# Five fixed PSUM places, earlier additions of finished sums, and means multiplied on GpSimd, in a graph network kernel

## The chip, the cores and the metric

The kernel runs on one core of one Trainium2 chip. The metric is device time in microseconds (us) of one execution. The kernel before took 1561.95 us, the median of three runs (1561.57 to 1563.52). A core has five engines that each work through their own queue in order: TensorE (PE; PEld is its weight load), VectorE (DVE), ScalarE (ACT), GpSimd (POOL) and SyncE (SP). They meet only through semaphores. Lines such as L1570 are lines of the kernel before; the change moves later lines down by 19 to 27.

## What is computed

A graph with 6250 nodes (64 features, `x`) has 206,250 directed edges (64 features each), sorted by destination `dst`; `src` says to which node an edge's message is added.

```python
msg = concat([x[dst], edge_attr], axis=1)          # 206250 x 128
h = relu(msg @ W1a.T + b1a) @ W1b.T + b1b          # 128, then 64
sums = segment_sum(h, src, 6250); counts = segment_sum(1, src, 6250)
agg = sums / maximum(counts, 1)
z = relu(concat([x, agg]) @ W2a.T + b2a) @ W2b.T + b2b
out = layernorm(x + concat([z, x]) @ Wr.T + br)    # no scale, eps 1e-5
```

All of it is float32. Because the second linear layer of the messages commutes with the mean, the kernel sums the 128 hidden values per node and applies the product `W1b`, `W2a` once per node.

## The kernel before

The 206,250 edges make 124 blocks of 13 tiles (a tile is 128 edges). For each block TensorE makes the hidden rows of its edges (`hidden`, L1385) into PSUM, and ScalarE applies the relu and writes them to an output row buffer `orow` in SBUF (L1389), a ring of four blocks. VectorE and TensorE meanwhile count, with one-hot matrices of bins (a bin is 128 nodes, there are 49), where each edge's row belongs in a large table `rows` in DRAM (`counts_of`, `bins_of`, `slots`). GpSimd then scatters each tile's 128 rows with one indirect DMA (`ones_`, L1436). In blocks 4 to 109 two or three times three tiles are "joined": edges of the same bin are put in fours (`marks` L1253, L1258, L1259, `join` L1288, `join_rows` L1300), and one indirect DMA writes 128 fours (`fours`, L1408). A block so takes 13, 9 or 7 scatters. Blocks 0 to 109 are epoch 0, then follow epoch 1 (12 blocks, 110 to 121) and epoch 2 (blocks 122 and 123), each with its own table; scatters of block k are issued after block k+2 is written in the program.

As soon as tiles of `rows` are full, SyncE reads them back (`read`, L1516) into a ring of nine buffers `rt`. VectorE makes one-hot matrices of the nodes (`nodes_of`, L1550), and TensorE sums a group of up to three bins with matmuls of 128x129 (`summed`, L1570) into one PSUM tile `g.ps`: the first half of a group in `sum_first`, the rest in `sum_rest`. The sums are added to `part` in SBUF by `collect(n)`, which leaves the n youngest finished groups for later: a first sum of a bin is copied by ScalarE (L1639), a later one is added by VectorE (L1641). In a joined block `sum_first` and `sum_rest` lie at both ends of the `join`, and `collect(0)` stands in the middle, behind `join_bases` on VectorE.

All PSUM tiles called `h_ps` come from one pool of five buffers, `hp`: hidden rows, joins, sums, and the products of the last rounds. A tile is requested under the same name each time and the pool hands out one of the buffers.

What is left after block 123 runs in this order: the sums of epoch 1, then the "last rounds": 17 groups of up to three bins, whose rows of epoch 2 are read and summed, with seven stages a group that are staggered over seven rounds. In round i the program handles `means` of group i-1 (VectorE, L1962 and L1963: one over the count), `scaled` i-1 (ScalarE, L1969: three scalings of 128x128), `turned` i-2 (three transposes on TensorE, L1976, and a copy by ScalarE, L1978), `layer` i-3 (TensorE L1982, VectorE maximum L1983), `residual` i-4 (TensorE L1988, VectorE add L1990), `squares` i-5 (ScalarE, L1997, three with a running sum), `written` i-6 (ScalarE root L2002, VectorE reciprocal L2003, multiply on GpSimd or, for the last two groups, on VectorE, L2006; SyncE stores it, L2011 and L2015), and the sums of group i. Six rounds without sums drain the stages.

The orders of TensorE, VectorE, ScalarE and SyncE are those of the program (`manual_schedule`, closed after the last rounds); GpSimd's is set by the framework. In blocks 9 to 122 most scatters also wait for a point that TensorE must have reached in the next block (`PACED`, `done`). At the very end a flag decides whether a general path runs; it doesn't here.

Of the kernel before, what the change touches and what calls it, by code (L numbers as in the profile page):

```python
# [8 lines left out]
F32 = mybir.dt.float32  # L9
# [4 lines left out]
AF = mybir.ActivationFunctionType  # L14
# [463 lines left out]
FULLQ = (3, 6, 9, 11, 13)  # L478
NODES = 8


# [7 lines left out]
def fast_path(  # L489
# [274 lines left out]
    with (  # L764
        tc.tile_pool(name="orow", bufs=1) as op,
        tc.tile_pool(name="oh", bufs=3) as ohp,
        tc.tile_pool(name="slotp", bufs=1, space=PSUM) as slpp,
        tc.tile_pool(name="hps", bufs=5, space=PSUM) as hp,
    ):
        by_slot = ctx.enter_context(ExitStack())  # L770
        rp = by_slot.enter_context(tc.tile_pool(name="rhs", bufs=1))
# [858 lines left out]
        def collect(n):  # L1630

            while len(totals) > n:
                g = totals.pop(0)
                to = part[:, g.b0 : g.b0 + g.nb, :]
                bins_ = range(g.b0, g.b0 + g.nb)
                assert len({b in begun for b in bins_}) == 1
                if g.b0 not in begun:
                    begun.update(range(g.b0, g.b0 + g.nb))
                    nc.scalar.copy(to, g.ps[:, : g.nb, :])  # L1639
                else:  # L1640
                    nc.vector.tensor_add(to, to, g.ps[:, : g.nb, :])  # L1641

        def sum_first(k):
# [4 lines left out]
            halves.append(g)  # L1648
            g.ps = hp.tile([P, SUMS, H + 1], F32, name="h_ps")
            g.half = range(g.b0, g.b0 + -(-g.nb // 2))  # L1650
# [122 lines left out]
        for k, ep_ in enumerate(epoch_of):  # L1773
# [11 lines left out]
            if joined(k):  # L1785
                marks(k, 0)
            if k == 1:
                join_consts()
# [21 lines left out]
            if after:  # L1810
                join_bases(k + 1)
            if joined(k):
                collect(0)
            for i in range(1, joined(k)):
# [133 lines left out]
        with tc.tile_pool(name="nw2", bufs=2) as nw2, tc.tile_pool(name="nw", bufs=3) as nw, tc.tile_pool(  # L1948
# [3 lines left out]
            class Nodes:  # L1952
# [13 lines left out]
                def scaled(self):  # L1966
                    self.agg = nw2.tile([P, SUMS, H], F32, name="agg")
                    for j in range(self.nb):
                        nc.scalar.activation(  # L1969
                            self.agg[:, j, :], part[:, self.b0 + j, :H], AF.Copy, scale=self.rc[:, j : j + 1]  # L1970
                        )

# [20 lines left out]
                def squares(self):  # L1993
                    self.ssq = nw.tile([P, SUMS], F32, name="ssq")
                    for j in range(self.nb):
                        sq = nw2.tile([P, D], F32, name="sq")
# [136 lines left out]
```

## Time and profile before

| what | value |
|---|---|
| median of three runs | 1561.95 us |
| the profiled execution | 1562.71 us |
| its span in the trace | 1560.9 us |
| TensorE busy | 1435.2 us, 92% |
| VectorE busy | 1369.4 us, 88% |
| GpSimd busy | 1134.2 us, 73% |
| ScalarE busy | 1120.6 us, 72% |
| mean granted TensorE clock | 0.972 |

The span begins with the first instruction and ends with the last; the execution's own time has 1.8 us around it. Busy time leaves out the issue of instructions, so an engine at 73% can be without a free moment: whether it is, the timeline tells, not the share. The chain of waits, which follows the end back to what released it, names TensorE for 64% of the span and DMA for 13%; it takes at each step one releaser and so says nothing of how much slack the others had. A group of the profile has count, busy us and mean ns, and the idle time ahead of it with what ended it.

### The profile page before, as it was taken

What the parts mean: (1) busy time and instruction counts of PE and PEld (TensorE: products, weight loads), DVE (VectorE), ACT (ScalarE), POOL (GpSimd) and SP (SyncE); (2) the same over time, 40 slices, a digit from 0 to 9 for tenths busy, and PEclk for the clock granted to TensorE, in tenths of its full rate; (3) what the DMA queues carried; (4) which work ended last, traced back from release to release, by engine and by line L of the source; (5) the groups of instructions that cost most, each with busy time, mean ns of one, the idle gap of its engine ahead of it and who ended that gap; (6) DMA issues with size and microseconds to landing.
All of it is one profiled execution on the core that took longest, in us unless ns stands there. A gap on an engine that the chain in (4) does not pass through costs nothing.

```text
span 1560.9 us, 33538 instructions
## 1 busy us (share of the span) xinstructions
PE 1435.2 (92%) x10958; PEld 1273.7 (82%) x10958; DVE 1369.4 (88%) x3031; ACT 1120.6 (72%) x2336; POOL 1134.2 (73%) x1215
## 2 busy tenths in 40 slices
PE   6688898879999899899998999999999999999896
PEld 5567777758888788788887888898888899999785
DVE  7589998979999899889998999999999888876786
ACT  3279999979888788787888878887877743432036
POOL 5777777777777777777777777777777777777711
PEclk9699999989999999999999999999999999999998
DMA  8878888868887888787787777676787899998873
GB/s 208 235 233 270 266 268 263 259 223 264 264 259 231 250 260 261 206 247 236 217 251 216 223 220 250 206 246 215 218 260 241 255 340 352 325 351 265 260 231 92
DMA packets 248713, 387.83 MB, mean 248 GB/s; under 512 B 43285, under 2 KB 180311, under 8 KB 248527
## 3 DMA queue, kind: packets, MB, share of 16 engines
q1 hardware_dynamic: 167661, 220.81, 50.4%
q0 software_dynamic: 47904, 122.68, 21.8%
q10 hardware_dynamic: 32962, 42.08, 8.1%
q8 instruction: 90, 1.47, 0.4%
q14 instruction: 96, 0.79, 0.2%
HBM read 214.09 MB, written 171.32 MB: 247 GB/s over the span
## 4 chain that ended last, share of the span: by engine, by line
PE 64%; DMA 13%; DVE 8%; ACT 7%; issue 4%; POOL 2%; SPq 0%; ACTq 0%; DVEq 0%; POOLq 0%
PE h_ps L1570 24%; PE h_ps L1288 13%; PE h_ps L1385 10%; PE h_ps L1300 8%; DMA rows<-orow,rowidx 8%; POOL rows L1436 2%; DMA rt<-rows 2%; DMA rows<-orow,qidx 1%; DVE marks L1253 1%; ACT marks L1258 1%; DVE oh L1550 1%; PE cnt_ps L1113 1%; ACT orow L1303 1%; PE cnt_ps L1114 1%; ACT orow L1389 1%
## 5 line engine op out<-in xcount | busy, mean ns | idle before, releaser
L1436 POOL DMA_INDIRECT rows<-orow,rowidx x922 | 898.7, 975 | 292.1 <-issue 143.0
L1570 PE MATMUL h_ps<-rt,oh 128*128 128x129 f32 x3952 | 487.3, 277 | 35.6 <-DVE oh L1550 9.9
L1570 PEld LDWEIGHTS h_ps<-rt,oh 128*128 128x128 f32 x3952 | 469.7, 193 | 49.6 <-issue 12.8
L1550 DVE TENSOR_TENSOR oh<-ramp,rt 128x768 f32<-128x768 bf16 (+4 forms) x391 | 308.2, 825 | 37.4 <-DMA rt<-rows 36.5
L1253 DVE TENSOR_TENSOR marks<-quad_ramp,ramp 128x1024 fp32r<-128x1024 f32 x230 | 276.6, 1209 | 0.0
L1408 POOL DMA_INDIRECT rows<-orow,qidx x230 | 224.0, 974 | 71.0 <-issue 25.9
L1385 PE MATMUL h_ps<-mv,rhs 124*128 124x128 f32 x1844 | 265.6, 289 | 4.4 <-ACT orow L1389 4.4
L1389 ACT ACTIVATE orow<-h_ps 128x512 f32<-128x512 f32 (+1 forms) x266 | 143.5, 539 | 173.5 <-PE h_ps L1385 163.8
L1288 PE MATMUL h_ps<-marks,side 128*128 128x512 f32 x690 | 261.7, 408 | 0.6 <-ACT mv L1354 0.6
L1300 PE MATMUL h_ps<-mv,rj 128*128 128x130 f32 x1840 | 236.7, 281 | 11.0 <-ACT orow L1389 7.4
L1385 PEld LDWEIGHTS h_ps<-mv,rhs 124*128 124x128 f32 x1844 | 233.2, 198 | 6.0 <-ACT orow L1389 4.6
L1288 PE MATMUL h_ps<-marks,rest 128*64 128x512 f32 x690 | 235.3, 395 | 0.0
L1300 PEld LDWEIGHTS h_ps<-mv,rj 128*128 128x128 f32 x1840 | 220.7, 193 | 16.9 <-ACT orow L1389 10.1
L1292 ACT COPY rj<-h_ps 128x512 f32<-128x512 f32 x230 | 131.5, 588 | 92.9 <-PE h_ps L1288 92.4
L1288 PEld LDWEIGHTS h_ps<-marks,side 128*128 128x128 f32 x690 | 131.0, 190 | 50.9 <-issue 2.1
L1259 ACT ACTIVATE marks<-marks,ones 128x512 fp32r<-128x512 f32 x230 | 166.1, 722 | 7.5
L1258 ACT ACTIVATE marks<-quad_ramp,z_act 128x512 fp32r<-128x512 f32 x230 | 166.0, 722 | 0.3 <-DVE z_act L1164 0.3
L1303 ACT ACTIVATE orow<-h_ps 128x260 f32<-128x260 f32 x460 | 151.4, 388 | 8.7 <-PE h_ps L1300 4.3
L1071 DVE TENSOR_TENSOR_SCAN had<-ramp,bins 128x400 bf16<-128x400 bf16 (+2 forms) x124 | 128.5, 1036 | 19.8 <-ACT bins L1092 6.4
L1338 ACT ACTIVATE rhs<-rhs,from_win 60x896 f32<-60x896 bf16 (+2 forms) x116 | 123.8, 1067 | 2.9
L1340 ACT ACTIVATE rhs<-rhs,ones 60x896 f32<-60x896 f32 (+2 forms) x116 | 123.5, 1065 | 2.9
L1288 PEld LDWEIGHTS h_ps<-marks,rest 128*64 128x64 f32 x690 | 93.7, 136 | 38.1 <-issue 0.6
(195 smaller groups left out, 1603.4 us busy)
## 6 DMA issues: line engine op xcount, KB each, us to landing
rt<-rows SPq DMA_DIRECT2D x194, 390.0 KB
rt<-rows SPq DMA_DIRECT2D x97, 325.0 KB
rows<-padrow ACTq DMA_DIRECT2D x24, 1040.0 KB
rhs<-in_edgeT SPq DMA_DIRECT2D x88, 224.0 KB
enat<-in_edgeJ SPq DMA_DIRECT2D x88, 192.0 KB
rows<-orow,rowidx POOLq DMA_INDIRECT x922
rt<-rows SPq DMA_DIRECT2D x40, 260.0 KB
rt<-rows SPq DMA_DIRECT2D x48, 195.0 KB
```

The lines of the kernel that those rows point to most:

```text
L1253: nc.vector.tensor_tensor(m[:, :n, :], all_q[:, None, :].to_broadcast([P, n, QUAD * P]), z[:, :n, None].to_broadcast([P, n, QUAD * P]), op ...
L1258: nc.scalar.activation(m[:, t, :], all_q, AF.Square, bias=z_acts[k][:, i * JOIN + t : i * JOIN + t + 1], scale=-1.0)
L1259: nc.scalar.activation(m[:, t, :], m[:, t, :], AF.Relu, bias=ones[:, :1], scale=-1.0)
L1288: done[k, f"turn{i}"] = nc.tensor.matmul(ps[: w.shape[1], :], w, m[:, t, :], start=t + p == 0, stop=last and p == 1).ins.name
L1300: done[k, f"join{i}"] = nc.tensor.matmul(ps[:, j, :], rj[:, (g0 + j) * P : (g0 + j + 1) * P], m, start=True, stop=True).ins.name
L1303: nc.scalar.activation(mrow[:, g0 : g0 + 2, :], ps, AF.Relu)
L1385: done[k, c] = nc.tensor.matmul(ps[:, j, :], rhs[:WIDE, of * P : (of + 1) * P], m[:WIDE, :H], start=True, stop=True).ins.name
L1389: nc.scalar.activation(orow_of(k, k0, n)[:, :, :H], ps[:, :n, :], AF.Relu)
L1408: s = nc.gpsimd.indirect_dma_start(out=qep.rows.rearrange("(q r) f -> q (r f)", r=QUAD), out_offset=bass.IndirectOffsetOnAxis(ap=qidx[:, q ...
L1436: s = nc.gpsimd.indirect_dma_start(out=ep_.rows, out_offset=bass.IndirectOffsetOnAxis(ap=rowidx[:, k % RING * BLK + j : k % RING * BLK + j ...
L1550: nc.vector.tensor_tensor(res[:, at_tile : at_tile + nb * n, :], ramp[:, None, :].to_broadcast([P, nb * n, P]), node[:, :, None].to_broadc ...
L1570: m = nc.tensor.matmul(of_bin(b), oh[:, at, :], rows, start=i == 0, stop=i == len(of) - 1)
```

## The change

Three parts, with one addition in the last.

1. The pool `hps` now holds five tiles of a whole bank each, made once. A class `Places` hands out views of them: `tile` takes the place that was longest unused (the front of a list) and puts it at the end of the list; for a sum, `kept` takes it out of the list, and `collect` puts it back when the sum has been added. TensorE's and SyncE's rows keep their sequence. Of TensorE's instructions 262 waited on TensorE's own semaphore before (115 of them at L1300, 71 at L1385, 64 at L1570), and one does now.
2. In a joined block `collect(0)` stands at the block's beginning, behind the first `marks`, no longer behind `join_bases`.
3. In the last rounds `scaled` is one GpSimd multiply of a whole group instead of up to three scalings on ScalarE. And of the last five groups, two (the fourth and the second from the end) get their squares on VectorE, as a multiply and a reduce.

```diff
--- before.py
+++ after.py
@@ -477,6 +477,7 @@
 ON_ACT = 1
 FULLQ = (3, 6, 9, 11, 13)
 NODES = 8
+BANK = 512
 
 
 def order_of(ngr):
@@ -765,8 +766,26 @@
         tc.tile_pool(name="orow", bufs=1) as op,
         tc.tile_pool(name="oh", bufs=3) as ohp,
         tc.tile_pool(name="slotp", bufs=1, space=PSUM) as slpp,
-        tc.tile_pool(name="hps", bufs=5, space=PSUM) as hp,
+        tc.tile_pool(name="hps", bufs=1, space=PSUM) as hpp,
     ):
+        class Places:
+
+
+            def __init__(self, n):
+                self.free = [hpp.tile([P, BANK], F32, name=f"h_ps{i}") for i in range(n)]
+
+            def tile(self, shape, dtype, name, hold=False):
+                place = self.free.pop(0)
+                if not hold:
+                    self.free.append(place)
+                if len(shape) == 2:
+                    return place[:, : shape[1]]
+                return place[:, : shape[1] * shape[2]].rearrange("p (a b) -> p a b", b=shape[2])
+
+            def kept(self, shape):
+                return self.free[0], self.tile(shape, F32, "h_ps", hold=True)
+
+        hp = Places(5)
         by_slot = ctx.enter_context(ExitStack())
         rp = by_slot.enter_context(tc.tile_pool(name="rhs", bufs=1))
         slp = by_slot.enter_context(tc.tile_pool(name="slot", bufs=2))
@@ -1639,6 +1658,7 @@
                     nc.scalar.copy(to, g.ps[:, : g.nb, :])
                 else:
                     nc.vector.tensor_add(to, to, g.ps[:, : g.nb, :])
+                hp.free.append(g.place)
 
         def sum_first(k):
 
@@ -1646,7 +1666,7 @@
                 mark()
             g = marked.pop(0)
             halves.append(g)
-            g.ps = hp.tile([P, SUMS, H + 1], F32, name="h_ps")
+            g.place, g.ps = hp.kept([P, SUMS, H + 1])
             g.half = range(g.b0, g.b0 + -(-g.nb // 2))
             work, done[k, "first"] = summed(g.reads, g.oh, lambda b: g.ps[:, b - g.b0, :], g.half)
             if not joined(k):
@@ -1784,6 +1804,7 @@
                 carried(k + 2)
             if joined(k):
                 marks(k, 0)
+                collect(0)
             if k == 1:
                 join_consts()
             if k == 0:
@@ -1809,8 +1830,6 @@
                 g = sum_first(k) if due > 0 else None
             if after:
                 join_bases(k + 1)
-            if joined(k):
-                collect(0)
             for i in range(1, joined(k)):
                 marks(k, i)
             if after:
@@ -1965,10 +1984,10 @@
 
                 def scaled(self):
                     self.agg = nw2.tile([P, SUMS, H], F32, name="agg")
-                    for j in range(self.nb):
-                        nc.scalar.activation(
-                            self.agg[:, j, :], part[:, self.b0 + j, :H], AF.Copy, scale=self.rc[:, j : j + 1]
-                        )
+                    nc.gpsimd.tensor_tensor(
+                        self.agg[:, : self.nb, :], part[:, self.bins, :H],
+                        self.rc[:, :, None].to_broadcast([P, self.nb, H]), op=ALU.mult,
+                    )
 
                 def turned(self):
                     tr = hp.tile([P, SUMS * P], F32, name="h_ps")
@@ -1992,6 +2011,14 @@
 
                 def squares(self):
                     self.ssq = nw.tile([P, SUMS], F32, name="ssq")
+                    if self.i + 5 >= len(last_groups) and (len(last_groups) - self.i) % 2 == 0:
+                        sq = nw2.tile([P, SUMS, D], F32, name="sqs")[:, : self.nb, :]
+                        y = self.y[:, : self.nb, :]
+                        nc.vector.tensor_tensor(sq, y, y, op=ALU.mult)
+                        nc.vector.tensor_reduce(
+                            self.ssq[:, : self.nb], sq, axis=mybir.AxisListType.X, op=ALU.add
+                        )
+                        return
                     for j in range(self.nb):
                         sq = nw2.tile([P, D], F32, name="sq")
                         nc.scalar.activation(sq, self.y[:, j, :], AF.Square, accum_out=self.ssq[:, j : j + 1])
```

VectorE at the beginning of a joined block with sums, before (`of_quads` and `bases` are those of `join_bases`, `part` is the addition of a finished sum):

```order
L1641 TENSOR_TENSOR part<-part,h_ps 128x387
L1253 TENSOR_TENSOR marks_155<-quad_ramp,ramp 128x1024
L1127 TENSOR_SCALAR of_quads_211<-cnt_ps 128x2x49
L1131 SCALAR_TENSOR_TENSOR bases_213<-of_quads_211,even 128x49 x2
L1641 TENSOR_TENSOR part<-part,h_ps 128x387
L1253 TENSOR_TENSOR marks_156<-quad_ramp,ramp 128x1024
```

and with the change:

```order
L1660 TENSOR_TENSOR part<-part,h_ps_132 128x387
L1272 TENSOR_TENSOR marks_160<-quad_ramp,ramp 128x1024
L1660 TENSOR_TENSOR part<-part,h_ps_131 128x387
L1146 TENSOR_SCALAR of_quads_216<-cnt_ps 128x2x49
L1150 SCALAR_TENSOR_TENSOR bases_218<-of_quads_216,even 128x49 x2
L1272 TENSOR_TENSOR marks_161<-quad_ramp,ramp 128x1024
```

The addition has moved ahead of the three instructions of `join_bases`; for bins that are summed for the first time the copy on ScalarE has moved forward in the same way.

ScalarE in two of the last rounds, before (`agg` the scaled means, `aT` their transpose, `rstd` the root, `sq` the squares):

```order
L1969 ACTIVATE agg<-part,rc 128x128 x3
L1978 COPY aT<-h_ps 128x384
L2002 ACTIVATE rstd<-ssq,eps 128x3
L1997 ACTIVATE sq,ssq<-y 128x64 x3
L1969 ACTIVATE agg<-part,rc 128x128 x3
L1978 COPY aT<-h_ps 128x384
L2002 ACTIVATE rstd<-ssq,eps 128x3
L1997 ACTIVATE sq,ssq<-y 128x64 x3
```

and with the change GpSimd's rows, from the first of the last rounds on:

```order
L1987 TENSOR_TENSOR agg<-part,rc 128x384 x6
L2033 TENSOR_TENSOR y<-y,rstd 128x192
L1987 TENSOR_TENSOR agg<-part,rc 128x384
L2033 TENSOR_TENSOR y<-y,rstd 128x192
L1987 TENSOR_TENSOR agg<-part,rc 128x384
L2033 TENSOR_TENSOR y<-y,rstd 128x192
```

The scalings have left ScalarE, where copy, root and squares stay in their order; on GpSimd they stand between the multiplies of the output, with the six of the first rounds ahead of all of those.

VectorE in the drain, with the change (before, the two rows of `sqs` were ScalarE's):

```order
L2009 TENSOR_TENSOR y<-h_ps_130,xr_14359 128x192
L2017 TENSOR_TENSOR sqs<-y 128x192
L2018 TENSOR_REDUCE ssq<-sqs 128x3
L2030 RECIPROCAL rstd<-rstd 128x3
L2002 TENSOR_TENSOR x_late_14345<-x_late_14345,h_ps_128 128x128
L2009 TENSOR_TENSOR y<-h_ps_129,xr_14360 128x192
```

The squares stand directly behind their own group's residual, ahead of the reciprocal of the group before and of the last group's maximum.

## The prediction

> **What bounds the kernel now.** I read the costliest groups first, then GpSimd's timeline, then its waits. Rows of the groups show count, then busy us and mean ns of one, then idle time ahead; timeline rows begin with start and length in us; wait rows give total us, times, longest.
>
> ```profile
> L1436 POOL DMA_INDIRECT rows<-orow,rowidx x922 | 898.7, 975 | 292.1 <-issue 143.0
> L1408 POOL DMA_INDIRECT rows<-orow,qidx x230 | 224.0, 974 | 71.0 <-issue 25.9
> ...
> 13.89 1.15 POOL L1436 DMA_INDIRECT rows<-orow,rowidx  x1 [9.25 <-ACT orow L1389]
> 15.34 0.97 POOL L1436 DMA_INDIRECT rows<-orow,rowidx  x1 [0.30 <-issue]
> 16.61 0.96 POOL L1436 DMA_INDIRECT rows<-orow,rowidx  x1 [0.30 <-issue]
> 59.82 1.37 POOL L1436 DMA_INDIRECT rows<-orow,rowidx  x1 [0.30 <-issue]
> ...
> 1489.46 0.97 POOL L1436 DMA_INDIRECT rows<-orow,rowidx  x1 [0.30 <-issue]
> ...
> POOL rows L1436 <- PE h_ps L1288: 13.0, 36, 1.2
> POOL rows L1408 <- ACT orow L1389: 4.8, 14, 0.9
> ```
>
> TensorE has the most busy time (92% of the span), but GpSimd is what never lets up. It issues 922 + 230 = 1152 scatters, and between two of them lie about 0.97 us of work and 0.30 us in which it waits for nothing the profile shows: a step of 1.27 us (15.34 to 16.61). The first starts at 13.89, the last at 1489.46: 1475.6 us for 1151 steps, and 1151 x 1.27 = 1461.8. Only 13.8 us are left for everything else. Of these, real waits are few: 36 waits of 13.0 us are 2.2 us more than 36 x 0.30, 14 of 4.8 us are 0.6 us more than 14 x 0.30, so about 2.8 us; the rest is scatters that themselves took longer, like the one of 1.37. So up to 1490 us the end is set by the number of scatters, which the change leaves alone.
>
> How far are the other engines ahead of GpSimd? L1376 is ScalarE's first write into a block's output rows; it must wait until the scatters of four blocks earlier have freed them.
>
> ```profile
> 1119.36 0.19 ACT L1376 CAST orow<-lo 128x7 f32<-128x7 bf16 x1
> ...
> 1144.26 0.97 POOL L1436 DMA_INDIRECT rows<-orow,rowidx  x1 [0.30 <-ACT side L1267]
> ...
> ACT orow L1376 <- DMA rows<-orow,rowidx: 22.9, 14, 3.2
> ```
>
> The first row is that of block 100 (the 101st of 124 such rows), the second the first scatter of block 100 (counted by scatters: 13 a block, or 9 and 7 with two and three joints). The lead is 24.9 us, and 14 times ScalarE had to wait for the ring of output rows. Time that TensorE or VectorE gains before 1438 us turns into a longer wait there.
>
> After the scatters three stretches follow.
>
> ```profile
> 1459.52 3.46 DMA rt<-rows
> ...
> 1463.07 1.42 DVE L1550 TENSOR_TENSOR oh<-ramp,rt 128x768 f32<-128x768 bf16 x2 [6.21 <-DMA rt<-rows]
> ...
> 1490.00:1495.00 5.00, 4.85 (x44) 4.66 (x42) 3.73 (x7) 0.00 (x0) 0.43 (x1) 1.00 1.05 392
> ...
> 1516.00:1545.00 29.00, 28.02 (x203) 23.91 (x202) 26.22 (x91) 26.23 (x127) 5.57 (x11) 1.00 0.56 141
> ...
> 1536.29 0.49 PE L1976 MATMUL h_ps<-ident,agg 128*128 128x128 f32 x3
> 1536.62 0.83 PE L1570 MATMUL h_ps<-rt,oh 128*128 128x129 f32 x6
> 1537.29 0.78 PE L1988 MATMUL h_ps<-wzz_t,x_late 128*128 128x64 f32 x6
> 1537.90 0.86 PE L1982 MATMUL h_ps<-aT,wam_t 128*128 128x384 f32 x2
> 1538.61 0.49 PE L1976 MATMUL h_ps<-ident,agg 128*128 128x128 f32 x3
> ```
>
> First (1459 to 1505), the sums of epoch 1: its reads wait for the landed scatters of block 121, and then the DMA engines are full (the window's row: engine busy times PE, PEld, DVE, ACT, POOL, then clock, DMA share 1.05). Second (1507 to 1545), the last rounds, 17 groups of bins. Third, the drain. In a round TensorE goes from one matmul group to the next without idle time: 0.33 + 0.67 + 0.61 + 0.71 = 2.32 us from 1536.29 to 1538.61. VectorE (26.22 of 29) and ScalarE (26.23) are about as full, but TensorE alone already makes the round 2.32 us.
>
> **The change part by part.** *Five fixed places, and finished sums added earlier.* TensorE's and SyncE's orders stay row for row; 261 of 262 waits of TensorE on its own semaphore go. All this lies before 1438 us, under the lead of 24.9 us: worth nothing, at most the 2.8 us of GpSimd's real waits. In the last rounds a held place goes back before the next is taken, so a buffer is again reused after five takings: nothing. Does the earlier add wait? One block, as it now runs:
>
> ```profile
> 1115.92 1.50 PE L1570 MATMUL h_ps<-rt,oh 128*128 128x129 f32 x12
> 1117.65 1.21 DVE L1253 TENSOR_TENSOR marks<-quad_ramp,ramp 128x1024 fp32r<-128x1024 f32 x1
> ...
> 1119.39 0.40 DVE L1641 TENSOR_TENSOR part<-part,h_ps 128x258 f32<-128x258 f32 x1
> ```
>
> The sums are done at 1117.42, the marks end at 1118.86, so the add behind them finds its input 1.44 us old. It only pushes the running bases behind it 0.40 us later, and the lead covers that. If it didn't, 0.40 us in each of at most 106 joined blocks would be 42.4 us, of which the lead swallows 24.9.
>
> *The means on GpSimd.* ScalarE loses three scalings a group, and GpSimd gets one multiply of 128x384. In a full round TensorE keeps 2.32 us, so nothing there; what moves is the start and the end. First the price of the multiply and of the squares:
>
> ```profile
> L2006 POOL TENSOR_TENSOR y<-y,rstd x15: 505/507/508, 1517.7 to 1549.6; 128x192 f32<-128x192 f32 x15
> ...
> 1549.97 0.39 DVE L2006 TENSOR_TENSOR y<-y,rstd 128x192 f32<-128x192 f32 x1
> ...
> 1113.58 0.52 DVE L1212 TENSOR_REDUCE row<-cnt_ps 128x7 f32<-128x350 f32 x1
> 1115.49 0.26 DVE L1184 TENSOR_REDUCE s_q<-hit_q 128x2 f32<-128x100 f32 x1
> ```
>
> GpSimd's multiply of 192 elements took 0.507 us. For 384 the bounds are 0.51 (length costs nothing) and 1.01 (all of it does); I take 1.0, the cautious end, since VectorE's own times grow with the length too (0.26 for 100 elements, 0.52 for 350 in the reduces). The Trainium skill (GPSIMD Engine Reference, section 3.1) gives 2.6 cycles per element at 1.2 GHz for a two-input operation, which I turn into an estimate of 0.92 us; by it the sum below would be 0.1 us better. A group's squares on VectorE are a multiply near 0.39 and a reduce between 0.26 and 0.52, say 0.75 together.
>
> The start:
>
> ```profile
> 1506.90 0.99 ACT L1969 ACTIVATE agg<-part,rc 128x128 f32<-128x128 f32 x3 [66.96 <-DVE rc L1963]
> 1507.36 0.91 PE L1976 MATMUL h_ps<-ident,agg 128*128 128x128 f32 x3 [0.83 <-ACT agg L1969]
> 1508.23 0.98 ACT L1969 ACTIVATE agg<-part,rc 128x128 f32<-128x128 f32 x3 [0.34 <-DVE rc L1963]
> 1509.12 0.46 ACT L1978 COPY aT<-h_ps 128x384 f32<-128x384 f32 x1
> 1509.63 0.91 PE L1982 MATMUL h_ps<-aT,wam_t 128*128 128x384 f32 x2 [0.68 <-ACT aT L1978]
> ```
>
> Group 0's means are scaled by 1507.89, now by 1506.90 + 1.0 = 1507.90: no difference. Its transposes end near 1508.3, but the copy of them stands on ScalarE behind group 1's scaling and starts at 1509.12. Without that scaling the copy starts near 1508.5 and ends near 1508.95; TensorE's sums in between end near 1509.0. So the first layer starts near 1509.05 instead of 1509.63, after which TensorE is packed: -0.6 us, with 0 (multiply 0.6 us longer) and -0.7 (all of the wait of 0.68) as bounds.
>
> The end:
>
> ```profile
> 1540.81 0.99 ACT L1969 ACTIVATE agg<-part,rc 128x128 f32<-128x128 f32 x3
> 1541.70 0.45 ACT L1978 COPY aT<-h_ps 128x384 f32<-128x384 f32 x1
> 1542.21 0.91 PE L1982 MATMUL h_ps<-aT,wam_t 128*128 128x384 f32 x2 [0.57 <-ACT aT L1978]
> ...
> 1548.61 0.23 DVE L1990 TENSOR_TENSOR y<-h_ps,xr 128x64 f32<-128x64 f32 x1
> 1549.21 0.24 ACT L1997 ACTIVATE sq<-y 128x64 f32<-128x64 f32 x1
> 1550.47 0.23 DVE L2006 TENSOR_TENSOR y<-y,rstd 128x64 f32<-128x64 f32 x1
> 1552.95 0.33 SPq L2015 DMA_DIRECT2D out_dram<-y  x1
> ```
>
> The copy at 1541.70 starts the moment a scaling leaves ScalarE; its transposes were done near 1541.4, so the chain of the drain starts 0.3 us earlier. At its other end the last group's squares start 0.37 us after their input (1548.84 to 1549.21), behind squares that VectorE now makes. Against this, VectorE has 0.75 us of squares twice, ahead of other steps of the drain. I take -0.2 for the two together, bounds -0.4 and +0.4. The last store is issued 2.25 us after the last multiply ends (1550.70), so SyncE may keep some of all this: bound 0.
>
> Sum: -0.6 - 0.3 - 0.2 = -1.1 us. The profiled execution took 1562.71 us (span 1560.9, 1.8 around it), so it would take 1561.6; it stands 0.8 above the median of 1561.95, so I predict 1560.8 us.
>
> **The rivals.**
>
> A, the forecast: 1560.8, its own range 1559.6 to 1562.2.
>
> B, the drain gives it all back: VectorE's squares and SyncE's late stores hold the end, 1561.9. For it speaks the gap of 2.25 us before the last store; against it that the start's 0.6 us comes earlier than any of this. The Trainium skill (SBUF — State Buffer, Who interferes with whom) says that a VectorE operation with two SBUF inputs contends with a GpSimd operation that reads SBUF. The new squares have two; the other VectorE work of the rounds has one operand in PSUM. Held up behind one multiply of 0.507 us each, the two squares would lose 1.0 us, which is B's time too.
>
> C, GpSimd's waits go: with TensorE's own waits gone, the 2.8 us vanish too: 1560.8 - 2.8 = 1558.0. For it: the two wait rows name TensorE and ScalarE as what was late. Against it: what those engines have to do ahead of these scatters is the same as before, in the same order.
>
> D, slower: GpSimd's multiply doesn't fit the round. The next round's transposes need it, and GpSimd also has 0.51 us of output multiply a round, so it decides from 2.32 - 0.51 = 1.8 us. At 2.2 us each of some 15 rounds would be 0.4 us longer, +6.0, and the start 0.6 later instead of earlier: 1561.95 + 6.6 = 1568.5. Against it stands 0.507 us for half the elements.
>
> E, slower: the earlier add stalls VectorE in joined blocks. Up to 42.4 - 24.9 = 17.5 us: 1579.5. The input that is 1.44 us old speaks against it.
>
> **How the numbers follow.** A 0.66, B 0.08, C 0.14, D 0.07, E 0.05. About 0.2% (3.1 us) is what this kernel's timing can tell from no change; A and B lie inside it, C (1558.0) is faster by 0.25%, D and E are slower. So faster 0.14, same 0.74, slower 0.12. The range of 1558.0 to 1563.4 holds A, B and about half of C with 0.7 us of scatter between runs around them, and leaves out D, E and the rest of C, some 0.19.
>
> **What would show it.** The last scatter should still start within 3 us of 1489.5 and the step stay 1.27. The rounds should stay 2.32 us apart. GpSimd's multiply should show 0.9 to 1.0 us, ScalarE half empty between 1516 and 1545, the first layer of group 0 about 0.6 us earlier against its group's first sum. Rounds longer than 2.32 mean D; a wait of VectorE's add on TensorE's sums in joined blocks, and GpSimd waits after 400 us, mean E. I am wrong at the root if the scatters end more than 4 us earlier.

## The result

The changed kernel takes 1559.32 us (median of 15 runs, 1555.14 to 1561.24), the kernel before 1561.95 us beside it (15 runs, 1559.88 to 1565.48): a ratio of 0.9982, 95% interval 0.9975 to 0.9989, or -1.7 to -3.9 us. The forecast of 1560.8 was on the right side and 1.5 us too late. The profiled execution of the changed kernel has a span of 1556.2 us, 4.7 below that of before.

One thing must be known for the numbers below: on three of the five chips on which experiments ran, the kernel before itself took 1961 to 1963 us, not 1562; the times of those runs (e1 to e6, e8 to e11) are compared only with each other and with the kernel before on the same chip.

The groups of GpSimd's scatters, first of the changed kernel's page (count, busy us, mean ns, then the idle time ahead of them):

```profile
L1455 POOL DMA_INDIRECT rows<-orow,rowidx x922 | 899.2, 975 | 290.6 <-issue 150.7
L1427 POOL DMA_INDIRECT rows<-orow,qidx x230 | 224.8, 977 | 70.1 <-issue 23.5
```

Before, the idle time was 292.1 + 71.0 = 363.1 us, now it is 360.7: 2.4 us less. The busy time is 1.3 us more, since single scatters take longer or shorter from one execution to the next. Where the idle time went is seen in GpSimd's timeline of the kernel before; these are the rows between 236 and 303 us that waited for more than the usual 0.30 us:

```profile
240.26 0.97 POOL L1436 DMA_INDIRECT rows<-orow,rowidx  x1 [0.97 <-PE h_ps L1288]
261.05 0.97 POOL L1436 DMA_INDIRECT rows<-orow,rowidx  x1 [0.73 <-PE h_ps L1288]
280.45 1.02 POOL L1408 DMA_INDIRECT rows<-orow,qidx  x1 [0.63 <-ACT side L1268]
282.69 0.96 POOL L1436 DMA_INDIRECT rows<-orow,rowidx  x1 [1.22 <-PE h_ps L1288]
302.34 0.96 POOL L1408 DMA_INDIRECT rows<-orow,qidx  x1 [0.89 <-ACT orow L1389]
```

Beyond 0.30 each, that is 2.9 us. In the changed kernel one row is left there (two more lie ahead of this window, 0.37 us at 178.98 and 0.43 at 219.25):

```profile
240.44 0.97 POOL L1455 DMA_INDIRECT rows<-orow,rowidx  x1 [0.71 <-DMA rows<-orow,rowidx]
```

The names behind the arrows of these rows must not be taken for the cause: what the scatters really waited for is worked out below, under "Places worth nothing".

The end of the changed kernel, from its timeline: the last scatter, the last addition of epoch 1, the first layer of group 0, the last addition of all, the last multiply and the last store's issue.

```profile
1488.29 0.97 POOL L1455 DMA_INDIRECT rows<-orow,rowidx  x1 [0.30 <-issue]
...
1502.01 0.29 DVE L1660 TENSOR_TENSOR part<-part,h_ps 128x129 f32<-128x129 f32 x1 [0.34 <-PE h_ps L1589]
...
1506.90 0.91 PE L2001 MATMUL h_ps<-aT,wam_t 128*128 128x384 f32 x2
...
1538.94 0.29 DVE L1660 TENSOR_TENSOR part<-part,h_ps 128x129 f32<-128x129 f32 x1
...
1547.60 0.23 DVE L2033 TENSOR_TENSOR y<-y,rstd 128x64 f32<-128x64 f32 x1
...
1548.66 0.40 SPq L2042 DMA_DIRECT2D out_dram<-y  x1
```

The differences of these rows make the stages of the end. They are the best instrument of this case, because the first three of them come out equal to 0.1 us in the traces with the same code of the last rounds, on the chips that take 1962 us too; the exceptions are the 9.55 of e9 and the 32.26 of e11. The last two stages differ by up to 1.2 and 0.6 us between executions of the same code. In us; the last column is the sum from the last addition of epoch 1 to the end:

| trace | code of the last rounds | to first layer | to last addition | to end of last multiply | to last store's issue | to the end | sum |
|---|---|---|---|---|---|---|---|
| before | before | 5.54 | 32.04 | 9.03 | 2.25 | 7.95 | 56.81 |
| e1 | before | 5.51 | 32.05 | 9.02 | 1.21 | 7.43 | 55.22 |
| e3 | before | 5.52 | 32.05 | 9.02 | 1.09 | 7.54 | 55.22 |
| e8 | before | 5.51 | 32.05 | 9.03 | 1.59 | 7.94 | 56.12 |
| e4 | means alone, no places | 4.91 | 32.05 | 9.18 | 1.03 | 7.87 | 55.04 |
| e2 | means and squares, no places | 4.91 | 32.05 | 9.18 | 0.42 | 8.05 | 54.61 |
| e9 | means and squares, no places | 4.91 | 32.05 | 9.55 | 0.41 | 8.06 | 54.98 |
| changed | changed | 4.89 | 32.04 | 8.89 | 0.83 | 7.54 | 54.19 |
| e5 | changed | 4.83 | 32.05 | 8.89 | 1.15 | 8.15 | 55.06 |
| e10 | changed | 4.84 | 32.04 | 8.89 | 0.87 | 8.12 | 54.87 |
| e11 | changed | 4.89 | 32.26 | 8.88 | 0.58 | 7.78 | 54.39 |
| e7 | changed, last stores from ScalarE | 4.89 | 32.04 | 9.83 | 0.03 | 6.35 | 53.14 |
| e12 | changed, last stores behind the last root | 4.89 | 32.06 | 8.88 | 0.18 | 7.27 | 53.28 |

The means of the sums are 55.84 for the four traces with the last rounds of before and 54.63 for the four with the changed ones: -1.2 us, of which the first three stages, -0.62, 0.0 and -0.14, are firm. The rest hangs on the last two stages. The two profiled executions alone differ by 2.6 us here (56.81 and 54.19). What is left of the gain, if anything, lies ahead of these stages.

### The profile page after: what moved, and what is told of

It reads as the page before. It is cut to its first block, busy times and chain, and to the rows that moved or that the text cites. A ratio compares the mean times of both kernels' runs of the same rounds, so it can differ in the third digit from the quotient of the medians.

```text
span 1556.2 us, 33620 instructions
## 1 busy us (share of the span) xinstructions
PE 1434.0 (92%) x10958; PEld 1272.8 (82%) x10958; DVE 1368.5 (88%) x3035; ACT 1099.8 (71%) x2275; POOL 1148.6 (74%) x1232
## 4 chain that ended last, share of the span: by engine, by line
PE 58%; DMA 15%; DVE 12%; ACT 7%; issue 5%; POOL 2%; SPq 1%; ACTq 0%; DVEq 0%; POOLq 0%
PE h_ps L1589 22%; PE h_ps L1307 11%; PE h_ps L1404 9%; DMA rows<-orow,rowidx 9%; PE h_ps L1319 7%; DMA rt<-rows 3%; DVE marks L1272 2%; DMA rows<-orow,qidx 2%; POOL rows L1455 2%; DVE oh L1569 2%; ACT marks L1277 1%; ACT orow L1322 1%; PE cnt_ps L1132 1%; PE cnt_ps L1133 1%; ACT marks L1278 1%
## 5 line engine op out<-in xcount | busy, mean ns | idle before, releaser
L1455 POOL DMA_INDIRECT rows<-orow,rowidx x922 | 899.2, 975 | 290.6 <-issue 150.7
L1589 PE MATMUL h_ps<-rt,oh 128*128 128x129 f32 x3952 | 488.8, 278 | 34.4 <-DVE oh L1569 15.2
L1427 POOL DMA_INDIRECT rows<-orow,qidx x230 | 224.8, 977 | 70.1 <-issue 23.5
L1319 PE MATMUL h_ps<-mv,rj 128*128 128x130 f32 x1840 | 229.0, 278 | 9.4 <-ACT rj L1311 4.1
L1319 PEld LDWEIGHTS h_ps<-mv,rj 128*128 128x128 f32 x1840 | 216.6, 192 | 11.7 <-ACT orow L1408 5.8
L1322 ACT ACTIVATE orow<-h_ps 128x260 f32<-128x260 f32 x460 | 147.1, 392 | 6.4 <-PE h_ps L1319 2.7
```

Source lines behind the costliest of these rows:

```text
L1319: done[k, f"join{i}"] = nc.tensor.matmul(ps[:, j, :], rj[:, (g0 + j) * P : (g0 + j + 1) * P], m, start=True, stop=True).ins.name
L1322: nc.scalar.activation(mrow[:, g0 : g0 + 2, :], ps, AF.Relu)
L1427: s = nc.gpsimd.indirect_dma_start(out=qep.rows.rearrange("(q r) f -> q (r f)", r=QUAD), out_offset=bass.IndirectOffsetOnAxis(ap=qidx[:, q ...
L1455: s = nc.gpsimd.indirect_dma_start(out=ep_.rows, out_offset=bass.IndirectOffsetOnAxis(ap=rowidx[:, k % RING * BLK + j : k % RING * BLK + j ...
L1589: m = nc.tensor.matmul(of_bin(b), oh[:, at, :], rows, start=i == 0, stop=i == len(of) - 1)
```

## The experiments

### e1 to e4: the parts of the change alone

e1 takes the changed kernel and gives `scaled` and all squares back to ScalarE; e3 also puts `collect(0)` back behind `join_bases`. e4 is the kernel before with the GpSimd multiply, e2 the same with the squares on VectorE too.

```diff
# e1: the changed kernel without part 3
-                    nc.gpsimd.tensor_tensor(
-                        self.agg[:, : self.nb, :], part[:, self.bins, :H],
-                        self.rc[:, :, None].to_broadcast([P, self.nb, H]), op=ALU.mult,
-                    )
+                    for j in range(self.nb):
+                        nc.scalar.activation(
+                            self.agg[:, j, :], part[:, self.b0 + j, :H], AF.Copy, scale=self.rc[:, j : j + 1]
+                        )
...
-                    if self.i + 5 >= len(last_groups) and (len(last_groups) - self.i) % 2 == 0:
...
# e3: besides, part 2 undone
                 marks(k, 0)
-                collect(0)
...
+            if joined(k):
+                collect(0)
```

> The changed kernel with ScalarE scaling the means and making all squares again, so only the fixed places and the earlier add are left of the change. Theory 1 (the forecast: everything before the last rounds is covered by ScalarE's lead over GpSimd): ratio to the kernel before 1.0000 within 0.0005, the last scatter within 0.5 us of 1489.46. Theory 2 (part of GpSimd's waits of 2.8 us go when TensorE no longer waits for itself): ratio 0.9986 to 0.9993 (1.2 us by the last scatter, up to 2.1 with the sums of epoch 1), last scatter near 1488.3. Theory 3 (SyncE's late stores made the difference): 1.0000, and the last store still issued some 2 us after the last multiply.

> The kernel before with only the means on GpSimd and the squares of two groups on VectorE; places and add as before. Theory 1: the first layer 0.6 us earlier against the last add of epoch 1, the drain 0.5 us shorter, ratio 0.9993 (-1.1 us). Theory 2 (the gain came with the places): start as in theory 1 but no more than -0.8 us in all, ratio 0.9995 to 1.0000. Theory 3 (the last stores leave SyncE sooner because the last rounds changed): -0.65 at the start, -0.14 in the drain and -1.4 behind the last multiply, -2.2 us, ratio 0.9986.

> Only the five fixed places, the finished sums added behind the running bases as before. Theory 1: 1.0000 within 0.0005. Theory 2: if the places are what shortens GpSimd's waits, the same ratio as with places and add together (0.9986 to 0.9993); if it is the earlier add, 1.0000 here.

> The kernel before with only the means on GpSimd; all squares stay on ScalarE. Theory 1: start 0.6 us earlier and drain 0.3 us earlier, the last group's squares again behind the squares of the group ahead on ScalarE, which costs 0.2 to 0.4 against both parts together: -0.7 to -0.9 us, ratio 0.9994 to 0.9996. If the squares on VectorE cost more than they save (they took 0.35 and 0.69 us for the multiply, and 0.35 for the reduce), this one is as fast as both parts together or faster by 0.2 us.

All four fell on a chip where the kernel before takes 1961.19 us. Ratios: e1 1.0045 (1.0014 to 1.0077), e3 1.0040 (1.0010 to 1.0069), e2 1.0018 (0.9988 to 1.0048), e4 1.0026 (0.9992 to 1.0060). What is different there is read in e1. First GpSimd's scatters, from its page:

```profile
L1455 POOL DMA_INDIRECT rows<-orow,rowidx x922 | 895.6, 971 | 622.7 <-issue 215.6
```

A scatter takes as long as ever (971 ns), but GpSimd is idle for 622.7 us ahead of these, not 290.6. Then e1's waits (total us, times, longest):

```profile
PE h_ps L1589 <- issue: 99.7, 110, 6.2
...
POOL rows L1455 <- PE h_ps L1589: 84.4, 41, 5.4
POOL rows L1455 <- PE h_ps L1307: 79.0, 63, 1.9
```

At its sums TensorE stops 110 times, for up to 6.2 us, for nothing that the profile shows (in e12, on another chip, once for 0.2 us), and the views name TensorE for much of GpSimd's waiting. So GpSimd is not the bound there, and theories 1 and 2 can't be told apart by the time. With the places (e1 and e3) that chip takes 0.4% longer; why isn't settled, and e8 doesn't repeat it on another chip. What the runs do tell is in the table: the means on GpSimd bring the first layer 0.6 us nearer, with places or without. The drain of e2 missed its expectation: 9.18 us, 0.15 longer and not 0.5 shorter than before. The reason is seen in e9.

### e8 and e9: the two halves again

The edits of e1 and e2 once more.

> As e1_places_and_add, on a chip that gives the kernel before 1562 us. Theory 1 (covered by ScalarE's lead): ratio 0.9996 to 1.0004, last scatter within 0.5 us of 1489.46. Theory 2 (part of GpSimd's real waits of 2.8 us goes with the places): ratio 0.9986 to 0.9993 (-1.2 us by the last scatter, up to -2.1 with the sums of epoch 1), last scatter near 1488.3.

> As e2_last_rounds, on a chip that gives the kernel before 1562 us. Theory 1 (all of the gain is made in the last rounds): ratio 0.9980 to 0.9988 (the whole 0.9982, or -0.65 at the start, -0.14 in the drain and -1.4 behind the last multiply). Theory 2 (half of it came with the places): ratio 0.9990 to 0.9996 (-0.6 to -1.6 us). In both the first layer of group 0 stands 4.9 us behind the last add of epoch 1, not 5.5.

The chip was again one of the three: the kernel before takes 1963.47 us there, e8 1.0012 of it (0.9986 to 1.0038), e9 0.9998 (0.9975 to 1.0020). Neither differs from it clear of noise, and neither is a test of the two theories. The ratio of each half on a chip with 1562 us was not measured. e9 shows one thing of the drain. This is VectorE's last addition into `y`, in e9's timeline:

```profile
1944.62 0.22 DVE L1990 TENSOR_TENSOR y<-h_ps,xr 128x64 f32<-128x64 f32 x1 [0.97 <-DMA out_dram<-y]
```

`y` has five buffers, so the last group's addition needs the one whose store was issued five groups earlier. Here it comes 7.34 us behind the last addition of sums, in the changed kernel 6.34. It waits for that store to land. By the semaphores in the traces the store lands 2.4 to 2.9 us after its issue in e2, e4 and e9, where the addition waits for 0.60 to 0.97 us. In nine other traces, with places and without (the kernel before and e3 among them), it lands after 1.8 us and the addition doesn't wait (in e1 after 1.97, a wait of 0.14). Why the store is late in some executions stays open.

### e5 and e10: more work for GpSimd

```diff
+        spare = const.tile([P, P], F32, name="spare")
         def scatter(k):
...
+            nc.gpsimd.tensor_tensor(spare, ident, ident, op=ALU.mult)
```

> The changed kernel with one GpSimd multiply of 128x128 (0.40 us by its row in the last rounds) ahead of each block's scatters, 124 in all, its product used by nothing. Theory 1 (the scatters' number sets the time until 1490 us): every one of them lengthens the run, by 0.40 to 0.70 us each (with a gap of 0.30 us as between scatters), so +50 to +87 us and the last scatter 50 to 87 us later. Rival (TensorE's 92% sets the time and GpSimd has slack): under +10 us. On a chip on which the engines stall as in the first four runs (1961 us for the kernel before), where GpSimd waits for the others, theory 1 too expects less than +20 us.

> As e5_more_gpsimd, on a chip that gives the kernel before 1562 us. Theory 1 (the number of scatters sets the time until 1490 us): the last scatter and the end 50 to 87 us later (124 multiplies of 0.40 us, with or without 0.30 us ahead of each). Rival (TensorE's 92% sets the time): under +10 us.

The edit did not do what was meant: GpSimd's order is the framework's, and it put all 124 multiplies at the start. The source line's view of e10:

```profile
L1417 POOL TENSOR_TENSOR spare<-ident x124: 398/398/1060, 4.5 to 114.6; 128x128 f32<-128x128 f32 x124
```

That is 49 us of work ahead of the first hundred scatters or so. Times: 1993.28 (before 1962.57) and 1992.52 (before 1963.47), +30.7 and +29.1. The last scatters start at 1879.29 and 1879.14, in e1 and e8, which have the same code up to there, at 1856.84 and 1846.57. So even where GpSimd waits for others, 22 to 33 of 49 us stay; the rest was made up. The two times lie outside both expectations, under 10 or 20 us and over 50. That GpSimd has no slack at all on the faster chips was not tested this way.

### e6 and e11: less work for TensorE

```diff
# e6: every second product of the sums, up to block 110
+                if light:
+                    of = of[::2]
                 for i, (at, rows) in enumerate(of):
```
```diff
# e11: of each pair of products in join, only the first
-                for p, w in enumerate(of[::-1] if last else of):
-                    done[k, f"turn{i}"] = nc.tensor.matmul(
-                        ps[: w.shape[1], :], w, m[:, t, :], start=t + p == 0, stop=last and p == 1
-                    ).ins.name
+                done[k, f"turn{i}"] = nc.tensor.matmul(
+                    ps, of[0], m[:, t, :], start=t == 0, stop=last
+                ).ins.name
```

> The changed kernel with every second matrix product of the epoch sums left out up to block 110 (the sums are then incomplete): some 1000 products, about 127 us less TensorE work by their row (278.47 us for 2192). Theory 1: GpSimd is the bound, so at most the 2.8 us of its real waits are gained, -0 to -3 us, and the waits of 0.6 to 1.2 us for TensorE's first layer between 238 and 300 us are gone. Rival (TensorE is the bound): -60 to -127 us. On a chip on which the engines stall as in the first four runs, where GpSimd waits for TensorE, -30 to -130 us.

> The changed kernel without the second product of each pair that turns a joint's edges (690 of 128x512, the edges' own features less the side's; the joined messages are then incomplete): 175 us less TensorE work (350.31 us for 1380) between 76 and 1231 us. Theory 1 (GpSimd is the bound): 0 to -3 us, the real waits of GpSimd go and no more, and ScalarE's lead over the scatters grows no further since the ring of output rows holds it. Rival (TensorE is the bound): -60 to -175 us.

e6 took 7795.55 us: its counts are incomplete, which the kernel notices at its end, and it then computes everything by its general path. Only what lies ahead can be read: the last scatter starts at 1853.0, between 1846.57 and 1856.84 of e8 and e1, though TensorE had some 127 us less to do. e11 took 1956.98 in one run beside 1963.47 (1950.58 to 1972.90), with 175 us less; last scatter 1844.41. So the rival "TensorE's 92% set the time" falls, with -6.5 us against -60 to -175. It falls on a chip of 1963 us; on one of 1562 us it was not tried.

### e7: the last stores from ScalarE's queue

```diff
+                    on = nc.scalar if self.i + 2 >= len(last_groups) else nc.sync
                     if full > 0:
-                        nc.sync.dma_start(
+                        on.dma_start(
...
-                        nc.sync.dma_start(out[NF * P :], y[:REM, full, :])
+                        on.dma_start(out[NF * P :], y[:REM, full, :])
```

> The changed kernel with the three output stores of the last two groups issued from ScalarE's queue instead of SyncE's (ScalarE has nothing behind its last square root). Theory 3 (the end hangs on how late SyncE issues the last store: 2.25 us after the last multiply in the kernel before, 0.83 in the changed one): the last store is issued within 0.3 us of the last multiply's end, and the end comes 0.5 us earlier than in the changed kernel against its last multiply. Rival (the issue itself and the landing make that time, whatever the queue): the span ends 8.4 us after the last multiply as in the changed kernel (0.83 + 7.54), within 0.2 us.

1555.57 us, one run, on a chip where the kernel before takes 1562.17. ScalarE's own rows and its DMA issues (ACTq), at the end:

```profile
1545.15 0.30 ACT L2029 ACTIVATE rstd<-ssq,eps 128x3 f32<-128x3 f32 x1 [0.65 <-DVE rstd L2030]
...
1546.08 0.39 ACTq L2039 DMA_DIRECT2D out_dram<-y  x1
1546.57 0.29 ACT L2029 ACTIVATE rstd<-ssq,eps 128x1 f32<-128x1 f32 x1 [1.12 <-DVE y L2033]
...
1547.35 0.28 ACTq L2043 DMA_DIRECT2D out_dram<-y  x1
```

The last store is issued 0.03 us behind the last multiply (1547.32), as theory 3 expects, and the end comes 6.35 us after that. But the store of the group ahead now stands in front of the last square root, which waits for it: the drain grows from 8.89 to 9.83 us. Net, 53.14 us from the last addition of epoch 1 to the end, against 54.63.

### e12: the stores behind the last root, and the add where it was

```diff
                 marks(k, 0)
-                collect(0)
...
+            if joined(k):
+                collect(0)
...
                     nc.scalar.activation(rstd[:, :n], self.ssq[:, :n], AF.Sqrt, bias=eps, scale=1.0 / D)
+                    for store in kept:
+                        nc.scalar.dma_start(*store)
...
+                    if self.i + 2 == len(last_groups):
+                        kept.extend(stores)
+                        return
+                    for store in stores:
+                        (nc.scalar if self.i + 1 == len(last_groups) else nc.sync).dma_start(*store)
```

> The changed kernel with two edits at places far apart. First, the earlier add is undone (finished sums are added behind the running bases as before), the fixed places stay. Second, the stores of the last two groups are issued from ScalarE's queue, both behind ScalarE's last square root. The second edit: the drain keeps its 8.89 us from the last add to the last multiply, the last store is issued 0.1 us behind it, and the end comes 6.1 to 6.4 us after that, so 15.2 to 15.6 us from the last add to the end instead of 17.26, -1.7 to -2.0. If the stores' queue doesn't matter, 17.2 to 18.2. The first edit, on a chip that gives the kernel before 1562 us: if the places shorten GpSimd's waits between 238 and 303 us, they stay as in the changed kernel (under 0.8 us in all beyond the gap of 0.30) and the last scatter starts at 1487.0 to 1488.3; if it is the earlier add, the waits are back (2.5 to 3.0 us) and the last scatter starts near 1489.5. Ratio to the kernel before: 0.9963 to 0.9975 in the first case, 0.9978 to 0.9988 in the second.

1558.59 us beside 1564.12 on the same chip, ratio 0.9964 (0.9950 to 0.9978): faster than before by 3.4 to 7.8 us, and by the stages of the end 1.4 us faster than the changed kernel (53.28 against 54.63), with which it was not timed side by side. The drain keeps 8.88, but from the last addition to the end it is 16.33 us, not 15.2 to 15.6. What stands out there is the one store that SyncE still has late:

```profile
1548.78 1.04 SPq L2049 DMA_DIRECT2D out_dram<-y  x1
```

Its issue takes 1.04 us, not 0.37, and ends at 1549.82, behind the start of ScalarE's own last one (1549.53). By its semaphore it is also the last of all stores to land, at 1552.94. That this makes the end late is likely, not shown.

For the places, first GpSimd's groups in e12's page:

```profile
L1455 POOL DMA_INDIRECT rows<-orow,rowidx x922 | 900.5, 977 | 290.5 <-issue 146.8
L1427 POOL DMA_INDIRECT rows<-orow,qidx x230 | 224.3, 975 | 70.4 <-issue 23.8
```

And e12's rows between 218 and 303 us that wait for more than 0.31 us:

```profile
220.23 0.97 POOL L1455 DMA_INDIRECT rows<-orow,rowidx  x1 [1.11 <-PE h_ps L1307]
...
239.79 0.97 POOL L1427 DMA_INDIRECT rows<-orow,qidx  x1 [0.52 <-ACT rhs L1357]
260.50 0.97 POOL L1427 DMA_INDIRECT rows<-orow,qidx  x1 [0.33 <-DMA rows<-orow,qidx]
```

Between 238 and 303 us the waits stay as short as the first case expected, but a long one stands just ahead, at 220.23, of the kind that the kernel before has at 240 and 282 us. In all, e12's scatters wait 1.0 us beyond the usual gap, those of the changed kernel 0.6, of e7 0.3 and of the kernel before 2.9. The idle time ahead of the scatters is 360.9 us, against 360.7, 360.6 (290.5 + 70.1) and 363.1. So the earlier add isn't needed for the lower figure. That the places bring it is not shown: there is one trace of the kernel before to set against three, and the next section finds that these waits are not for TensorE.

The last scatter starts at 1489.34, which only the other case expected: the scatters themselves were 2.1 us longer in all than before (1124.8 against 1122.7), which hides the 2.2 us. Where the last scatter starts in one trace says little.

## Why the prediction was right, and where not

**The bound.** Right: the scatters keep their step, the last starts within 3 us of 1489.5, ScalarE's lead over block 100 is 24.7 us (24.9 before), and after 241 us no scatter of the changed kernel waits for more than 0.40 us. One reading in it was wrong, the names of the waits. A smaller one: of the 13.8 us that were left over, some 5.6 are not longer scatters but the gap, which is 0.305 us and not 0.30.

**Places worth nothing.** Nothing here refutes this step, and nothing shows that the places brought anything ahead of the last rounds. The forecast took from its two wait rows that TensorE and ScalarE kept GpSimd waiting for 2.8 us, and C was built on it. The traces say otherwise. The scatters report their landing on eight semaphores in turn, and each scatter starts behind the landing of the one eight earlier, which used the same semaphore. A landing takes 4.7 to 4.9 us (the median of each trace), and eight steps take 10.2 us, so as a rule it is long past. These are all scatters, behind the first one, that waited for more than 0.32 us in the four traces of chips with 1562 us:

| trace | scatters that waited | beyond the gap, in all | landing of the one eight earlier took | start behind that landing |
|---|---|---|---|---|
| before | 5 | 2.9 us | 9.8 to 10.7 us | 0.75 us each |
| changed | 3 | 0.6 us | 9.7 to 10.3 us | 0.75 us each |
| e7 | 1 | 0.3 us | 10.2 us | 0.27 us |
| e12 | 3 | 1.0 us | 9.8 to 10.5 us | 0.75 us each |

Eleven of twelve start at the same distance behind a late landing, whatever engine the row names: PE, ACT, DVE, DMA or none. A view names the semaphore that came last, and those of TensorE and ScalarE are counted up all the time (TensorE's five times between 282.3 and 283.8 us). The product of TensorE that the row at 282.69 of the kernel before names ended there at 282.53. In e7 the same product ended only at 283.88, and the same scatter had started at 281.20, behind the usual gap.

So C's 2.8 us were waits for late landings, and that TensorE no longer waits for itself can't remove them by the way that C thought of. Five landings were late in the kernel before, three, one and three in the other traces. Whether the change has a part in that or it is chance, one trace of the kernel before can't tell. The chips with 1962 us are no help: of the 273 waits over 0.32 us in e1 (behind the first eight scatters) none follows a landing in this way.

Whether the time ahead of the last rounds fell at all depends on what one takes for the end of the kernel before. With the mean of its four traces (55.84), the end accounts for -1.2 of the interval of -1.7 to -3.9 us, and -0.5 to -2.7 are left; of e12's -3.4 to -7.8 us, -0.8 to -5.2 are left. With its only trace on a chip of 1562 us (56.81), the end accounts for -2.2, and nothing need be left. The forecast of -1.1 lies outside the interval, and 1559.32 lies 0.3 us below A's own range, so the forecast lacks something, here or in the last stores. Which, stays open.

**The earlier add worth nothing.** In agreement with e12, where the idle time ahead of the scatters is the same without it. E fell: no 0.40 us per block anywhere.

**The start, -0.6.** Right: 5.52 to 4.9 us in all traces, -0.62, with places or without. The multiply took 0.827 us, not 1.0:

```profile
L1987 POOL TENSOR_TENSOR agg<-part,rc x17: 401/827/828, 1504.9 to 1539.9; 128x384 f32<-128x384 f32 x16, 128x128 f32<-128x128 f32 x1
```

That is less than the value taken. It is also less than the estimate of 0.92 that the prediction worked out from the Trainium skill (GPSIMD Engine Reference, section 3.1). The sum hangs little on it: the copy of group 0 no longer stands behind a scaling, as forecast. D fell with it: the rounds stay 2.32 us, 32.04 in all.

**ScalarE half empty.** Right, from 26.23 of 29 us to this (window's row; PE, PEld, DVE, ACT, POOL):

```profile
1515.00:1541.00 26.00, 25.66 (x188) 21.93 (x186) 23.70 (x82) 14.36 (x81) 14.59 (x23) 1.00 0.57 145
```

**The drain, -0.3 and -0.2.** From the last addition to the last multiply it is -0.14, not -0.5. The first term holds: the copy that stood at +0.03 us behind the last addition (1541.70 against 1541.67) now starts at 1538.72, -0.22. The second is the mis-sized one, and the profile shows by what. Two squares of the same size in the changed kernel, with a multiply of GpSimd beside the second:

```profile
1543.58 0.35 DVE L2017 TENSOR_TENSOR sqs<-y 128x192 f32<-128x192 f32 x1
...
1545.40 0.51 POOL L2033 TENSOR_TENSOR y<-y,rstd 128x192 f32<-128x192 f32 x1 [0.42 <-DVE rstd L2030]
1545.42 0.69 DVE L2017 TENSOR_TENSOR sqs<-y 128x192 f32<-128x192 f32 x1
...
1546.60 0.48 ACT L2029 ACTIVATE rstd<-ssq,eps 128x3 f32<-128x3 f32 x2 [0.65 <-DVE rstd L2030]
```

The second square takes 0.69 us, and the root on ScalarE stands behind it. So it is in every trace with such an overlap (0.68 to 0.69 in six), and 0.35 in every square without one (ten). In e2 GpSimd's multiply ended before the second square began:

```profile
1941.40 0.51 POOL L2014 TENSOR_TENSOR y<-y,rstd 128x192 f32<-128x192 f32 x1 [0.42 <-DVE rstd L2011]
...
1942.07 0.35 DVE L1998 TENSOR_TENSOR sqs<-y 128x192 f32<-128x192 f32 x1
```

That is B's mechanism, at 0.34 us on one of the two squares instead of 1.0 us on both. The Trainium skill (SBUF — State Buffer, Who interferes with whom) says that VectorE with two SBUF inputs contends with a GpSimd operation that reads SBUF; the traces agree. Without it the drain would have been some 0.5 us shorter, as forecast: an estimate from 0.14 + 0.34. No run shows it, since in e2 and e9 a late store lengthens the drain.

**SyncE may keep some.** It did not. From the last multiply to the last store it was 2.25, 1.21, 1.09 and 1.59 us with the last rounds of before, mean 1.5, and 0.83, 1.15, 0.87 and 0.58 with the changed ones, mean 0.9: -0.7, of which the way to the end took 0.2 back (7.7 and 7.9 in the mean). It hangs on single issues of stores that take 0.5 to 1.5 us instead of 0.37, near 8.3 us behind the last addition or later, in all traces looked at; why those issues take longer stays open. The executions differ by 0.6 to 1.2 us here, so this part is the least certain, and that the change brought it is not shown.

**The sums of epoch 1** had no term. From the last scatter to their last addition it was 14.63 us before, then 13.72 (changed), 13.53 (e7) and 14.18 (e12). It can look as if TensorE's waits for itself went there. But this wait of the kernel before (first row) has its twin in the changed one (second row), with another name behind the arrow:

```profile
1504.95 1.58 PE L1570 MATMUL h_ps<-rt,oh 128*128 128x129 f32 x12 [0.90 <-PE h_ps L1570]
...
1502.82 1.61 PE L1589 MATMUL h_ps<-rt,oh 128*128 128x129 f32 x12 [0.85 <-DVE oh L1569]
```

Both end 0.1 us behind VectorE's one-hot matrix (its ends: 1504.85 and 1502.76), and the later product needs it. One wait of TensorE lies within the stretch in the kernel before, 0.70 us at 1495.55, and none in the others. It too ends 0.1 us behind a signal of VectorE, whose one-hot had waited for its rows to be read back:

```profile
1494.49 1.68 DVE L1550 TENSOR_TENSOR oh<-ramp,rt 128x768 f32<-128x768 bf16 x2 [1.27 <-DMA rt<-rows]
```

With one trace of the kernel before, the 0.5 to 1.1 us are not proved.

So the sum of A's terms came out (-1.1 forecast, -1.2 measured), and in part by luck: the start was right, but the drain gave 0.4 less than forecast, and the stores, put at nothing, gave 0.5 more. What the forecast lacked beside that lies in the last stores or ahead of the last rounds, and its cause is open.

## What to carry to other kernels

A lead that one engine has late in a program says nothing of the stretch where it is built up: list the bound engine's real waits with their times before calling a change hidden. Before explaining such a wait by the engine that a view names, see whether the same distance lies behind the same event each time, and whether the named instruction ends at the same place in another run. And a short stage whose length is equal to 0.1 us in nearly every trace tells more of a sub-microsecond edit than the time of the whole kernel.

## What the runs showed of the hardware that was not expected

The same program takes 1562 us on two chips of the experiments and 1962 us on three, with the same lengths of single operations (scatters of 971 and 975 ns) and idle time between them on every engine. The mean granted clock of the kernel before is 0.91 to 0.93 on the three and 0.97 to 0.98 on the two. What makes the engines stop was not found.

GpSimd's multiply took 0.40, 0.51 and 0.83 us for 128, 192 and 384 elements, about 1.7 ns an element and 0.2 us besides. A square of 128x192 on VectorE took 0.35 us alone and 0.69 beside such a multiply.

An indirect scatter landed 4.7 to 4.9 us after its start in the median. Up to 303 us some took 10 us, as long as eight steps of GpSimd, and the scatter eight later then waited for up to 0.9 us beyond the usual gap.
